# Four 32-column tiles of the matmul array for the layer-3 products of a four-layer graph attention kernel

## The chip, the cores and the metric

The kernel runs on one core of one Trainium2 chip. The metric is the device time of one execution in microseconds (us). Runs of one kernel agree here within about 0.2%.

The profile shows four engines at work. In the kernel before, TensorE (PE) has 12678 matmuls and as many weight loads (PEld), VectorE (DVE) 4595 instructions, ScalarE (ACT) 3009 and GpSimd (POOL) 1455. I call the operand of a weight load the stationary one and the other the moving one: in the rows of line 526 they are 128x65 (LDWEIGHTS) and 128x512 (MATMUL).

## The reference, cut to what matters

Sixteen graphs of 1024 nodes with 256 features go through four attention layers. The first three have one head of 256 values. The fourth, layer 3, has four heads of 64:

```python
h = jnp.einsum('bnd,hde->bhne', nodes_embed, W)            # 4 heads, 64 values each
...
weight = jnp.where(node_adj[:, None] == 0, NEG, weight)
attention = jax.nn.softmax(weight, axis=-1)
dst = jnp.einsum('bhij,bhje->bhie', attention, h) + bias[None, :, None, :]
out = jax.nn.relu(dst) + h                                 # then a norm per head
```

The softmax is done as a weighted sum divided by the sum of the weights. So each target node needs 64 sums of values and one sum of weights per head. These products are in f32.

## The kernel before

Two streams of batches run interleaved: even and odd batches are Python generators. They yield a planned cost, and the one with less planned time is advanced next. `LAG` is the planned start of the second stream. A scheduler then fixes the order of the instructions on each engine.

The weights of a head are eight tiles of 128 source nodes by 1024 targets, made by VectorE (line 317). Layer 3 multiplies them in line 526. The 65 columns of `V3` (64 values and the weight factor) are the stationary operand, and half of the targets is the moving one:

```python
for n in range(H * NH):                       # 4 heads x 2 halves of the targets
    h, g = divmod(n, NH)
    ...
    accT = accumulator(b)[: E + 1, :]         # 65 partitions x 512
    for j in range(NI):                       # 8 source blocks
        if n == 0:
            next(behind)                      # VectorE: the next block's weights
        nc.tensor.matmul(                     # line 526
            accT, V3[:, j, h, :], weights[h * NI + j][:, ts(g, HALF)],
            start=(j == 0), stop=(j == NI - 1),
        )
        ...
    nc.scalar.copy(sums, accT)
    ...
    for i in range(NG):                       # back to targets on partitions
        nc.tensor.transpose(acc[:, i, :], sums[:, ts(i, P)], ident[: E + 1, : E + 1])
    inverse(inv, acc[:, :, E])
    nc.vector.tensor_mul(y[:, ts(g, NG), h, :], acc[:, :, :E], inv...)
```

Of the kernel before, what the change touches and what calls it, by code (L numbers as in the profile page):

```python
# [32 lines left out]
F32 = mybir.dt.float32  # L33
# [5 lines left out]
ALU = mybir.AluOpType  # L39
AX = mybir.AxisListType  # L40

P = 128
# [17 lines left out]
def short_path(ctx: ExitStack, tc: tile.TileContext, ins: dict, out: bass.AP, bad: bass.AP):  # L60

    nc = tc.nc
    x, adj = ins["x"], ins["adj"]
    B, N, D = x.shape
    H, T, E = ins["L3_a_src"].shape
    NI = N // P
    NK = D // P
    HALF = 512
    NH = N // HALF
    NG = HALF // P  # L70
    EXT = [3, 3, 3, 3 * H]
    LAG = 120.0
    ROOT_D = D**0.5
    ROOT_E = E**0.5

# [3 lines left out]
    wide = ctx.enter_context(tc.tile_pool(name="wide", bufs=2))  # L79
    psum = ctx.enter_context(tc.tile_pool(name="psum", bufs=2, space=bass.MemoryType.PSUM))  # L80
    dram = ctx.enter_context(tc.tile_pool(name="dram", bufs=1, space=bass.MemoryType.DRAM))

    ident = const.tile([P, P], F32, name="ident")
# [23 lines left out]
    def load(b: int):  # L107


        narrow = narrows[b % 2]  # L110
        rows = narrow.bitcast(U8).rearrange("(c t q) j -> c q t j", t=2, q=P)
        for c in range(NI // 2):
            cast = nc.gpsimd.dma_start(
                rows[c], adj[b, ts(c, 2 * P), :].rearrange("(q t) j -> q t j", t=2)
            )
            tc.keep_in_program_order(cast)
        if b < 2:
            fetch_nodes(b)
        yield

        mask = masks[b] = nodes.tile([P, NI // 2, N, 2], U8, name="mask")
        for c in range(NI // 2):
            turn = nc.sync.dma_start_transpose(
                mask[:, c].rearrange("p n t -> p (n t)").bitcast(BF), narrow[:, ts(c, P)]
            )
            tc.keep_in_program_order(turn)
            yield
        if b > 1:
            fetch_nodes(b)
            yield  # L130

    def test(b: int):

        for i in range(NI):

            adj_i = adjs.tile([P, N], BF, name="adj_i")
            fetch = nc.gpsimd.dma_start(adj_i, adj[b, ts(i, P), :])  # L137
            if b == 0:
                tc.keep_in_program_order(fetch)


            square = nc.scalar.activation(  # L142
                adj_i, adj_i, AF.Square, bias=minus_half, accum_out=squares[:, b, i : i + 1]
            )
            tc.keep_in_program_order(square)
            yield
# [4 lines left out]
    small = ctx.enter_context(tc.tile_pool(name="small", bufs=6))  # L151
# [104 lines left out]
    def inverse_root(squared: bass.AP, n: int, elements: int, eps: float) -> bass.AP:  # L256

        r = small.tile([P, n], F32, name=f"rstd{n}")
        nc.gpsimd.tensor_scalar_add(r, squared, elements * eps)  # L259
        nc.gpsimd.tensor_tensor(r, r, minus_half.to_broadcast([P, n]), op=ALU.pow)  # L260
        return r

    def accumulator(b: int) -> bass.AP:
        return psum.tile([P, HALF], F32, name=f"acc{b % 2}")
# [40 lines left out]
    def weigh(b: int, column, c, op, into: list):  # L305


        while row_taken:
            yield 0.25
        row_taken.append(b)  # L310
        r = psum.tile([P, N], F32, name="row", bufs=1)
        for i in range(NI):
            nc.tensor.transpose(r[:, ts(i, P)], column(i).to_broadcast([P, P]), ident)  # L313
        yield 0.5
        for j in range(NI):
            w = edges.tile([P, N], F32, name=f"weights{b % 2}")
            nc.vector.scalar_tensor_tensor(w, r, c(j), masks[b][:, j // 2, :, j % 2], op0=op, op1=ALU.mult)  # L317
            into.append(w)
            if j == NI - 1:
                row_taken.pop()  # L320
            yield 0.5

    def start(behind, b: int):

        for t in behind:
            if row_taken == [b]:
                return
            yield t

    def inverse(inv: bass.AP, total: bass.AP):  # L330

        nc.vector.tensor_scalar_max(inv, total, TINY)  # L332
        nc.vector.reciprocal(inv, inv)  # L333
# [14 lines left out]
    def batch(b: int):  # L348
# [3 lines left out]
        coming = load(b + 2) if b + 2 < B else iter(())  # L352
        testing = test(b)
# [18 lines left out]
        last = {}  # L372
# [84 lines left out]
        sums = small.tile([P, NI], F32, name="sums_of_x")  # L457
# [16 lines left out]
        V3 = yield from attend(2, V, finish, 3)  # L474
# [3 lines left out]
        y = single.tile([P, NI, H, E], F32, name="y")  # L478
        normed = []
        shape = [P, NI, E]  # L480

        def center(h: int):

            yh = y[:, :, h, :]
            head = ts(h, E)
            nc.gpsimd.tensor_add(yh, yh, bias[:, head].unsqueeze(1).to_broadcast(shape))  # L486
            nc.vector.scalar_tensor_tensor(yh, yh, 0.0, h3[:, :, head], op0=ALU.max, op1=ALU.add)  # L487
            mean = small.tile([P, NI], F32, name="mean")
            nc.vector.tensor_reduce(mean, yh, AX.X, ALU.add)
            nc.vector.tensor_scalar_mul(mean, mean, 1.0 / E)  # L490
            nc.vector.tensor_sub(yh, yh, mean.unsqueeze(2).to_broadcast(shape))
            square = wide.tile(shape, F32, name="wide", bufs=1)
            nc.scalar.activation(square, yh, AF.Square)
            var = small.tile([P, NI], F32, name="var")
            nc.vector.tensor_reduce(var, square, AX.X, ALU.add)
            return yh, head, inverse_root(var, NI, E, L3_EPS)

        def rescale(yh: bass.AP, head, rstd: bass.AP):
            nc.vector.tensor_mul(yh, yh, rstd.unsqueeze(2).to_broadcast(shape))
            nc.gpsimd.tensor_mul(yh, yh, gamma[:, head].unsqueeze(1).to_broadcast(shape))  # L500
            nc.gpsimd.tensor_add(yh, yh, xb[:, :, head])

        weights = []

        def weigh3(h: int):
            if h == H:
                return iter(())
            return weigh(
                b, lambda i: ex[:, i, 2 * H + h : 2 * H + h + 1],
                lambda j: ex[:, j, H + h : H + h + 1], ALU.max, weights,  # L510
            )

        behind = weigh3(0)
        yield from start(behind, b)
        for n in range(H * NH):
            h, g = divmod(n, NH)
            if g == NH - 1:

                behind = weigh3(h + 1)
                yield from start(behind, b)  # L520

            accT = accumulator(b)[: E + 1, :]
            for j in range(NI):
                if n == 0:
                    next(behind)
                nc.tensor.matmul(  # L526
                    accT, V3[:, j, h, :], weights[h * NI + j][:, ts(g, HALF)],
                    start=(j == 0), stop=(j == NI - 1),
                )
                if n > 0:  # L530
                    next(behind, None)
                yield 0.9
            for _ in behind:
                pass
            sums = wide.tile([E + 1, HALF], F32, name="sums")
            nc.scalar.copy(sums, accT)  # L536
            next(testing)
            next(coming, None)
            yield 0.5
            acc = psum.tile([P, NG, E + 1], F32, name="misc")  # L540
            for i in range(NG):
                nc.tensor.transpose(acc[:, i, :], sums[:, ts(i, P)], ident[: E + 1, : E + 1])  # L542
            inv = small.tile([P, NG], F32, name="inv4")
            inverse(inv, acc[:, :, E])
            nc.vector.tensor_mul(
                y[:, ts(g, NG), h, :], acc[:, :, :E], inv.unsqueeze(2).to_broadcast([P, NG, E])
            )
            yield 0.5
            if g == NH - 1:
                if h > 0:  # L550
                    rescale(*normed.pop())
                normed.append(center(h))
                yield 1.0
        for _ in coming:
            pass
        rescale(*normed.pop())
# [8 lines left out]
    def stream(first: int):  # L565
        for _ in loading[first]:
            yield 2.0
        for b in range(first, B, 2):
            yield from batch(b)
# [3 lines left out]
    next(preparing)  # L573
    streams = [[0.0, stream(0)], [LAG, stream(1)]]
    while streams:
# [311 lines left out]
def tile_gat4(  # L887
# [27 lines left out]
    nc.vector.memset(ones, 1.0)  # L915
    n_bad = flags.tile([1, 1], I32, name="n_bad")
    short_path(tc, ins, out, bad)
    with tc.tile_pool(name="flag_psum", bufs=1, space=bass.MemoryType.PSUM) as psum:
        bads = psum.tile([1, 1], F32, name="bads")
# [39 lines left out]
```

## Time and profile before

The median is 3115.27 us (3113.33 to 3118.95, three runs).

A pass is one matmul instruction of the trace. Each f32 product of layer 3 shows as two passes: 1024 products, 2048 passes.

| what | before |
|---|---|
| TensorE busy | 96% of the span, 98% in mid-kernel |
| VectorE busy | 68% |
| passes of the layer-3 product | 2048, 0.429 us apart |
| passes of layers 0 to 2 (line 408) | 6144, 0.217 us apart |
| TensorE waiting for VectorE's weights | 34 us in all |

A busy TensorE says little about what a change of its work is worth, because matmuls overlap: one of line 526 lasts 592 ns, and the next starts after 429. What counts is the distance between the starts of successive passes. The prediction shows these lines and reads them.

I use one account throughout. I took the start times of all matmuls of a trace and charged each pass the spacing that it has in a dense stream. Each edge between tiled and ordinary passes is charged as read further down, and what remains between the starts counts as waits. The rest of the span lies before the first and after the last matmul. For the kernel before: 2899.3 us of streaming, 177.2 of waits and 38.1 outside, together 3114.6 of a span of 3114.5.

### The profile page before, as it was taken

Reading aid. Unit: us, or ns where it says so; the run is one execution under the profiler, and the core shown is the slowest. Engines: PE = TensorE matmul, PEld = TensorE weight load, DVE = VectorE, ACT = ScalarE, POOL = GpSimd, SP = SyncE. Lnnn points to the kernel's source line nnn. Section 1 sums busy time; section 2 is a strip of 40 time slices with the busy share of each in tenths; the row PEclk is TensorE's granted clock in tenths of the full one; section 3 lists DMA queues with packets and bytes.
Section 4 is the critical chain, followed back from the end, with each engine's and each line's share of the span. In section 5 each row is a group of like instructions: output and inputs, shape, how many; then the busy total and the mean of one; then the engine's idle time right before and its main releaser. Section 6 shows DMA issues by size and latency. Waiting matters only on the chain.

```text
span 3114.5 us, 36472 instructions
## 1 busy us (share of the span) xinstructions
PE 2991.3 (96%) x12678; PEld 2054.2 (66%) x12678; DVE 2113.3 (68%) x4595; ACT 1112.7 (36%) x3009; POOL 961.1 (31%) x1455
## 2 busy tenths in 40 slices
PE   7999999999999999999999999999999999999985
PEld 6775766767576576766757667675765757667552
DVE  5666686666866658676675866768667585766755
ACT  2433334343342433424333343432424334343331
POOL 2123323233242323323233232332323233232333
PEclk9999999999999999999999999999999999999998
DMA  7103122030222203122031220302212131010101
GB/s 124 31 7 52 37 29 53 8 48 28 31 51 21 36 29 45 35 27 55 4 48 31 28 55 7 46 30 31 51 17 38 31 45 34 14 29 4 21 20 26
DMA packets 120462, 105.58 MB, mean 34 GB/s; under 512 B 73680, under 2 KB 91216, under 8 KB 120272
## 3 DMA queue, kind: packets, MB, share of 16 engines
q0 software_dynamic: 40448, 67.12, 14.7%
q1 hardware_dynamic: 79824, 36.05, 5.3%
q8 instruction: 103, 1.69, 0.2%
q14 instruction: 87, 0.71, 0.1%
HBM read 153.49 MB, written 33.55 MB: 60 GB/s over the span
## 4 chain that ended last, share of the span: by engine, by line
PE 76%; DVE 15%; ACT 3%; POOL 3%; issue 3%; DMA 1%; SPq 0%; DVEq 0%; ACTq 0%; POOLq 0%
PE acc L408 36%; PE acc L526 22%; PE acc L296 12%; DVE weights L317 8%; PE misc L289 3%; PE row L313 2%; ACT square L280 1%; PE misc L542 1%; POOL y L486 1%; DVE V L364 1%; DVE x_b L344 1%; POOL rstd L260 1%; DVE x_b L343 1%; ACT below L340 1%; DVE y L487 1%
## 5 line engine op out<-in xcount | busy, mean ns | idle before, releaser
L408 PE MATMUL acc<-V,weights 128*128 128x257 f32 x6144 | 1458.7, 385 | 45.5 <-DVE weights L317 32.5
L408 PEld LDWEIGHTS acc<-V,weights 128*128 128x128 f32 x6144 | 1148.1, 191 | 365.9 <-DVE weights L317 113.7
L526 PE MATMUL acc<-weights,V 128*65 128x512 f32 x2048 | 955.3, 592 | 1.9 <-DVE weights L317 1.5
L317 DVE SCALAR_TENSOR_TENSOR weights<-row,ex,mask 128x1024 f32<-128x1024 f32 x512 | 629.6, 1278 | 11.4 <-PE row L313 11.0
L296 PE MATMUL acc<-W,hT 128*128 128x259 f32 (+1 forms) x2048 | 512.9, 389 | 21.1 <-ACT hT L291 12.9
L526 PEld LDWEIGHTS acc<-weights,V 128*65 128x65 f32 x2048 | 273.3, 138 | 363.0 <-issue 316.4
L317 DVE SCALAR_TENSOR_TENSOR weights<-row,V,mask 128x1024 f32<-128x1024 f32 x384 | 479.6, 1278 | 46.2 <-PE row L313 46.2
L296 PEld LDWEIGHTS acc<-W,hT 128*128 128x128 f32 x2048 | 379.3, 191 | 141.2 <-ACT hT L291 45.6
L280 ACT ACTIVATE square<-x_b,minus_mean 128x256 bf16<-128x256 f32 x512 | 261.0, 510 | 299.7 <-DVE minus_mean L270 288.0
L340 ACT ACTIVATE below<-acc,inv 128x256 f32<-128x256 f32 x256 | 121.1, 473 | 639.7 <-DVE inv L333 517.3
L260 POOL TENSOR_TENSOR rstd<-rstd,minus_half 128x2 f32<-128x2 f32 (+1 forms) x320 | 302.0, 944 | 21.9
L137 POOL DMA_DIRECT2D adj_i<-in_adj_dram x128 | 77.6, 606 | 640.6 <-ACT adj_i L142 628.9
L259 POOL TENSOR_SCALAR rstd<-squared 128x2 f32<-128x2 f32 x256 | 63.3, 247 | 587.4 <-ACT square L280 587.3
L291 ACT ACTIVATE hT<-misc 128x512 f32<-128x512 f32 x256 | 148.4, 596 | 224.9 <-PE misc L289 224.3
L332 DVE TENSOR_SCALAR inv<-acc 128x1 f32<-128x1 f32 x256 | 39.1, 156 | 274.0 <-PE acc L408 272.0
L273 DVE TENSOR_SCALAR centered<-x_b,minus_mean 128x256 f32<-128x256 f32 x512 | 163.7, 365 | 60.2 <-PE misc L289 56.3
L343 DVE SCALAR_TENSOR_TENSOR x_b<-below,x_b 128x256 f32<-128x256 f32 x256 | 125.3, 489 | 103.2 <-ACT below L340 102.9
L360 ACT ACTIVATE V<-acc,rstd 128x3 f32<-128x3 f32 x384 | 99.5, 262 | 244.0 <-PE acc L296 243.8
L289 PEld LDWEIGHTS misc<-ident,centered 128*128 128x128 f32 x1024 | 123.5, 141 | 83.8 <-issue 44.5
L289 PE MATMUL misc<-ident,centered 128*128 128x128 f32 x1024 | 153.7, 276 | 17.3 <-DVE centered L273 17.3
L364 DVE TENSOR_SCALAR V<-acc,rstd,V 128x256 f32<-128x256 f32 x256 | 134.6, 541 | 48.5 <-ACT V L360 47.8
L536 ACT COPY sums<-acc 65x512 f32<-65x512 f32 x128 | 74.1, 579 | 247.2 <-PE acc L526 247.2
(73 smaller groups left out, 2166.4 us busy)
## 6 DMA issues: line engine op xcount, KB each, us to landing
adj_i<-in_adj_dram POOLq DMA_DIRECT2D x128, 256.0 KB, 3.9
x_b<-in_x_dram SPq DMA_DIRECT2D x16, 1024.0 KB, 6.5
narrow<-in_adj_dram POOLq DMA_DIRECT2D x64, 256.0 KB, 9.4
out_dram<-y POOLq DMA_DIRECT2D x32, 512.0 KB, 7.6
mask<-narrow SPq DMA_TRANSPOSE x64, 3.9
W<-in_L_gnn_W_dram SPq DMA_DIRECT2D x3, 256.0 KB, 6.3
weights<-in_L_gnn_a_dram SPq DMA_DIRECT2D x3, 256.0 KB, 8.0
W<-in_L_gnn_W_dram SPq DMA_DIRECT2D x2, 128.0 KB, 7.9
```

Of the source, the lines that this page charges most:

```text
L260: nc.gpsimd.tensor_tensor(r, r, minus_half.to_broadcast([P, n]), op=ALU.pow)
L273: nc.vector.tensor_scalar(centered[:, n, :], xb[:, 2 * pair + n, :], minus_mean[:, n : n + 1], 0.0, op0=ALU.add, op1=ALU.max,)
L280: nc.scalar.activation(square, xb[:, 2 * pair + n, :], AF.Square, bias=minus_mean[:, n : n + 1], accum_out=squared[:, n : n + 1],)
L289: nc.tensor.transpose(turned[:, k, ts(n, P)], centered[:, n, ts(k, P)], ident)
L291: nc.scalar.mul(hT, turned, ROOT_D)
L296: nc.tensor.matmul(projected, hT[:, k, ts(n, P)], W[l][:, k, :], start=(k == 0), stop=(k == NK - 1),)
L317: nc.vector.scalar_tensor_tensor(w, r, c(j), masks[b][:, j // 2, :, j % 2], op0=op, op1=ALU.mult)
L340: nc.scalar.activation(below, acc[:, :D], AF.Exp, scale=inv)
L343: nc.vector.scalar_tensor_tensor(xi, below, 1.0, xi, op0=ALU.min, op1=ALU.add)
L364: nc.vector.tensor_scalar(V[:, i, :D], projected[:, :D], rstd, V[:, i, D : D + 1], op0=ALU.mult, op1=ALU.mult,)
L408: nc.tensor.matmul(accs[i], weights[j][:, ts(i, P)], V[:, j, : D + 1], start=(j == 0), stop=(j == NI - 1),)
L526: nc.tensor.matmul(accT, V3[:, j, h, :], weights[h * NI + j][:, ts(g, HALF)], start=(j == 0), stop=(j == NI - 1),)
```

## The change

The 65-column product (128*65 in the page) is half as wide as those of line 408 (128*128). After the change the array is addressed as four tiles of 32 columns. Each source block gives four products of 32 values (two halves of the targets, two halves of the values), one per tile. The sums of weights become products of their own, with the weight column broadcast to 32. Four source blocks' products are emitted together. The planned units are adapted, so `LAG` goes from 120 to 111.

```diff
-    LAG = 120.0
+    LAG = 111.0
+    QUAD = P // 4
...
+        def in_tiles(parts, accT: bass.AP, first: bool, last: bool):
+            for n, (values, moving) in enumerate(parts):
+                made = nc.tensor.matmul(
+                    accT[ts(n, QUAD), :], values, moving, start=first, stop=last
+                )
+                if pinned:
+                    tc.keep_in_program_order(made)
+                pinned.append(made)
...
+        def add_values(h: int, j: int):
+            for n in (j + 1, j):
+                parts = [
+                    (V3[:, n, h, ts(e, QUAD)], moving)
+                    for moving in halves_of(h, n)
+                    for e in range(2)
+                ]
+                in_tiles(parts, acc, n == 1, n == NI - 2)
+        def add_totals(h: int, j: int):
+            parts = [
+                (V3[:, j + n, h, E:].to_broadcast([P, QUAD]), halves_of(h, j + n)[g])
+                for g, n in ((0, 1), (0, 0), (1, 1), (1, 0))
+            ]
+            in_tiles(parts, total, j == 0, j == NI - 2)
...
+            step = 4
+            for first in range(0, NI, step):
+                pinned = []
+                for j in range(first, first + step, 2):
+                    add_totals(h, j)
+                    if h > 0:
+                        add_values(h, j)
+                for _ in range(step):
+                    next(behind, None)
+                yield 1.8 if h == 0 else 5.4
```

The two accumulators (`acc`, `total`) are then copied, transposed as full 128-row tiles, and normalised once per head on VectorE instead of once per half.

More of the change, by code (lines that the diff above doesn't have):

```diff
@@ L511, in weigh3, with halves_of @@
             )
+        def in_tiles(parts, accT: bass.AP, first: bool, last: bool):
[6 more added lines that the diff above has]
+                pinned.append(made)
+        def halves_of(h: int, j: int):
+            return [weights[h * NI + j][:, ts(g, HALF)] for g in range(NH)]
@@ L513, in batch @@
         behind = weigh3(0)
         yield from start(behind, b)
-        for n in range(H * NH):
-            h, g = divmod(n, NH)
-            if g == NH - 1:
-                behind = weigh3(h + 1)
-                yield from start(behind, b)
-            accT = accumulator(b)[: E + 1, :]
-            for j in range(NI):
-                if n == 0:
-                    next(behind)
-                nc.tensor.matmul(
-                    accT, V3[:, j, h, :], weights[h * NI + j][:, ts(g, HALF)],
-                    start=(j == 0), stop=(j == NI - 1),
-                )
-                if n > 0:
+        for h in range(H):
+            acc = accumulator(b)
+            total = accumulator(b)
+            if h == 0:
+                for j in range(0, NI, 2):
+                    next(behind)
+                    next(behind)
+                    pinned = []
+                    add_values(h, j)
+                    yield 1.8
+                for _ in behind:
+                    pass
+            behind = weigh3(h + 1)
+            yield from start(behind, b)
+            step = 4
+            for first in range(0, NI, step):
+                pinned = []
+                for j in range(first, first + step, 2):
+                    add_totals(h, j)
+                    if h > 0:
+                        add_values(h, j)
+                for _ in range(step):
@@ L531, in batch @@
                     next(behind, None)
-                yield 0.9
+                yield 1.8 if h == 0 else 5.4
             for _ in behind:
                 pass
-            sums = wide.tile([E + 1, HALF], F32, name="sums")
-            nc.scalar.copy(sums, accT)
-            next(testing)
-            next(coming, None)
+            copies = []
+            for accT in (acc, total) if h == 0 else (total, acc):
+                copies.append(wide.tile([P, HALF], F32, name="sums"))
+                nc.scalar.copy(copies[-1], accT)
+                next(testing)
+                next(coming, None)
@@ L539, in batch @@
+            sums, totals = copies if h == 0 else copies[::-1]
             yield 0.5
-            acc = psum.tile([P, NG, E + 1], F32, name="misc")
+            turned = psum.tile([P, NG, P], F32, name="misc")
             for i in range(NG):
-                nc.tensor.transpose(acc[:, i, :], sums[:, ts(i, P)], ident[: E + 1, : E + 1])
-            inv = small.tile([P, NG], F32, name="inv4")
-            inverse(inv, acc[:, :, E])
+                nc.tensor.transpose(turned[:, i, :], totals[:, ts(i, P)], ident)
@@ L545, in batch @@
+            inv = small.tile([P, NH, NG], F32, name="inv8")
+            nc.vector.tensor_reduce(
+                inv, turned[:, :, ::QUAD].rearrange("p i (g n) -> p g i n", n=2), AX.X, ALU.add
+            )
+            inverse(inv, inv)
+            turned = psum.tile([P, NG, NH, E], F32, name="misc")
+            for i in range(NG):
+                nc.tensor.transpose(
+                    turned[:, i].rearrange("p g e -> p (g e)"), sums[:, ts(i, P)], ident
+                )
             nc.vector.tensor_mul(
-                y[:, ts(g, NG), h, :], acc[:, :, :E], inv.unsqueeze(2).to_broadcast([P, NG, E])
+                y[:, :, h, :].rearrange("p (g i) e -> p g i e", g=NH),
+                turned.rearrange("p i g e -> p g i e"),
+                inv.unsqueeze(3).to_broadcast([P, NH, NG, E]),
@@ L547, in batch @@
             )
             yield 0.5
-            if g == NH - 1:
-                if h > 0:
-                    rescale(*normed.pop())
-                normed.append(center(h))
-                yield 1.0
+            if h > 0:
+                rescale(*normed.pop())
+            normed.append(center(h))
+            yield 1.0
         for _ in coming:
```

## The prediction

The prediction's charge for switching is the author's estimate: of the 592 ns of a pass of line 526, 592 - 429 = 163 ns lie under its successor, and entering and leaving the tiling are each charged with these, 0.326 us a run. The kernel before has no tiled pass, so neither this nor the overlap of tiles could be read from its trace, and the 15% for tiles that do not overlap is a judgement.

> **What bounds the kernel now.** I read the engine shares first, then a stretch in mid-kernel, then the groups, then the chain, and the waits last.
>
> The shares and three groups of the page:
> ```profile
> PE 2991.3 (96%) x12678; PEld 2054.2 (66%) x12678; DVE 2113.3 (68%) x4595; ACT 1112.7 (36%) x3009; POOL 961.1 (31%) x1455
> ...
> L408 PE MATMUL acc<-V,weights 128*128 128x257 f32 x6144 | 1458.7, 385 | 45.5 <-DVE weights L317 32.5
> ...
> L526 PE MATMUL acc<-weights,V 128*65 128x512 f32 x2048 | 955.3, 592 | 1.9 <-DVE weights L317 1.5
> ...
> L526 PEld LDWEIGHTS acc<-weights,V 128*65 128x65 f32 x2048 | 273.3, 138 | 363.0 <-issue 316.4
> ```
> TensorE is busy for 96% of the span and the next engine, VectorE, for 68%. Line 526 is the layer-3 product, the one the change rewrites. It needs 16 batches x 4 heads x 2 halves x 8 blocks = 1024 products, and the row has 2048 instructions: an f32 product runs as two passes, each with its own weight load. The row also shows the waste: 128*65 means that 65 of the array's 128 columns are used.
>
> Four hundred microseconds in the middle, all instructions, then line 526 alone (columns: stretch, its length, busy time of each engine):
> ```profile
> 1000.00:1400.00 400.00, 392.08 (x1672) 268.98 (x1671) 282.53 (x608) 145.07 (x392) 128.86 (x192) 1.00 0.23 36
> ...
> 1000.00:1400.00 400.00, 129.90 (x279) 37.42 (x280) 1.00 0.23 36
> ```
> In steady state TensorE is busy for 98% at full clock, and a third of that is line 526. Two batches run interleaved, so one batch's layer 3 lies beside another's earlier layers.
>
> A busy time from modelled ends is not a cost. The cost is the distance from one start to the next, and the chain that ended last gives it (start, length, what):
> ```profile
> 1440.59 4.29 PE acc L526 x10
> ...
> 1493.91 6.93 PE acc L408 x32
> ...
> 1528.94 0.87 PE row L313 x8
> ```
> 4.29 / 10 = 0.429 us for a pass of 512 moving columns, 6.93 / 32 = 0.217 us for 257, and 0.109 us for a transpose of 128. A matmul's own duration is 592 ns, so 592 - 429 = 163 ns of each lies under its successor. Line 526 thus costs 2048 x 0.429 = 879 us of TensorE. TensorE does wait for someone, but little:
> ```profile
> PE acc L408 <- DVE weights L317: 32.5, 41, 1.7
> PE misc L289 <- DVE centered L273: 17.3, 16, 12.0
> PE acc L296 <- ACT hT L291: 12.9, 21, 1.0
> ```
> So a microsecond taken from the TensorE stream should come off the end nearly whole, until VectorE's 68% comes near.
>
> [...]
>
> **The change part by part.**
>
> *Removed:* 1024 full-array products, 2048 passes, 879 us. Also 512 transposes of a 65-row tile, whose 65 moving columns follow each other at about 60 ns: 31 us.
>
> *Added, streaming:* per head, each of 8 source blocks gives four products of 32 values (two halves of the targets by two halves of the 64 values). The sums of weights, formerly the 65th column, become products of their own: 2 halves x 8 blocks, with the weight column broadcast to 32. That is 32 + 16 = 48 products, dealt to four tiles, or 12 per tile, two passes each. If the four tiles stream together a head needs 24 pass times instead of 32. Over 64 heads the ideal is 64 x 24 = 1536 pass times. The scheduler cuts some groups of four apart. I counted in the compiled changed program, run of tiled passes by run, the passes on the fullest tile: 1606 in all. 1606 x 0.429 = 689 us. The transposes become 512 of 128 columns: 512 x 0.109 = 56 us. Stream balance: 689 + 56 - 879 - 31 = -165 us.
>
> *Added, switching:* the compiled program has 324 separate runs of tiled passes, about 20 a batch. The lengths are mostly 8, 16 and 48 passes: four source blocks are held together in heads 1 to 3, but head 0 is fed block by block as VectorE makes the weights, and other work cuts in between. Every run enters and leaves the tiling. [...] A first load may be exposed as well. Loads are 138 ns for 65 columns and 191 for 128 (the LDWEIGHTS rows), so by straight line about 111 for 32. Worst case: 0.33 + 0.11 + 0.19 = 0.63 us a run, 204 us in all. With hidden loads: 324 x 0.326 = 106 us. I take this second figure, because the trace shows loads hidden everywhere else. It is a choice, not a measurement.
>
> *VectorE:* per head before, two of each: a clamp at 156 ns, a reciprocal at 176, a multiply of 256 elements at 421, or 1.51 us. After: one reduction of some 0.25 us (estimate, from the 172 ns of the smallest reductions), clamp and reciprocal 0.33, one multiply of 512 at 0.69 (as the other 512-element operations): 1.27 us. That is 64 x 0.24 = 15 us less, off the path. ScalarE still copies two tiles of 512 per head at 579 ns. GpSimd does not change.
>
> *Moved:* before, a head used one accumulator at a time and the other was being filled. Now values and totals hold both, so this stream's next head waits for one or two copies (0.58 us each). The other stream usually fills that time. I charge 15 us for 64 heads, about 0.23 us each.
>
> Sum: -165 + 106 + 15 = -44 us, so 3071 us, rounded to 3070. The shift of the second stream's start (120 to 111 in the program's own planning units) is half of the shortened plan of a batch, and I give it nothing by itself.
>
> **The rivals.**
>
> *Tiles do not overlap[...].* In the compiled program the two passes of a product stand side by side on the same tile: first pass tile 0, second pass tile 0, first pass tile 1, and so on. If matmuls must also start in program order, the second pass of tile 0 holds back tile 1, and only two passes overlap. Counted over the same 324 runs that is 3400 pass times, 1459 us instead of 689, and the kernel would take over 3700 us. [...] a plan that holds 24 products together makes little sense without overlap. Some 15%.
>
> *Switching eats the gain.* With 0.51 us a run the 165 us are gone; with 0.63 us the kernel is 3115 - 165 + 204 + 15 = 3169 us. For it: 324 runs are many, and those in head 0 contain only two groups of four. [...]
>
> *Switching is almost free*, only the stream counts: 3115 - 165 + 15 = 2965 us. That is the good end; the waits of TensorE on VectorE would grow a little, as VectorE rises to about 71%.
>
> *VectorE becomes the bound:* 2098 us of work against 2965 says no over the whole. Locally, eight weight rows at 1.28 us are 10.2 us a head, against 10.3 us of ideal tiled streaming, so head 0 may wait. That would show as tens of microseconds at most.
>
> **Range and chances.** Independent tiles with cheap to dear switching give 2965 to 3169. [...] The in-order case lies far above, or partly so if overlap is imperfect. I put the range at 2945 to 3300, which leaves room below for better packing between the two streams and cuts off the far tail. Faster by over 2% (below 3053): 0.42. Within 2%: 0.33. Slower by over 2% (above 3178): 0.25.
>
> **What would show it.** Tiles together: within a held run the four tiles' passes start close together, and 24 products span about 12 x 0.429 = 5.1 us; 10 us or more would mean the in-order rival. Switching: the gap between the last tiled pass's start and the next full-array start beyond 0.429 us, and the reverse on entering; I expect some 0.16 us each. Line 408 must keep 0.217 us a pass and the granted clock must stay at 1.00, or another effect is at work. Waits of TensorE on the weights should remain below 60 us. The prediction is wrong if tiled passes on different tiles space out at 0.2 us or more, or if a switch costs above 0.5 us.

## The result

The changed kernel takes 3024.82 us (3023.68 to 3025.67, four runs) against 3114.86 us in the same rounds. The ratio is 0.9709 (95% interval 0.9692 to 0.9726): faster by 2.9%. Ratios are the mean time of one kernel's fast runs over that of the other's of the same rounds, so not quite the ratio of the medians. The prediction had 3070 us. The measured time is inside its range, but the forecast gain of 45 us was half of the real 90 us.

The shares and the same groups of the page of the changed kernel (line 517 is now the layer-3 product, 409 is the old 408):
```profile
PE 2905.2 (96%) x16774; PEld 1960.1 (65%) x16774; DVE 2112.7 (70%) x4467; ACT 1092.1 (36%) x3009; POOL 964.5 (32%) x1455
...
L409 PE MATMUL acc<-V,weights 128*128 128x257 f32 x6144 | 1452.5, 386 | 24.6 <-ACT above L343 12.8
...
L517 PE MATMUL acc<-weights,V 128*32 128x512 f32 x6144 | 756.4, 598 | 3.6 <-DVE weights L318 3.6
...
L517 PEld LDWEIGHTS acc<-weights,V 128*32 128x32 f32 x6144 | 174.1, 109 | 379.6 <-issue 370.6
```
The layer-3 product now has three times as many passes, each as long as before (598 against 592 ns), and is busy for 756 us instead of 955. One after the other, 6144 passes at 0.429 us would take 2636 us, so passes run at the same time. The loads of 32 columns take 109 ns, where the prediction had estimated 111. TensorE is still busy for 96%, and 78% of the chain that ended last lies on it (76% before).

The same stretch in mid-kernel, all instructions and then line 517 alone:
```profile
1000.00:1400.00 400.00, 393.26 (x2321) 261.66 (x2320) 284.40 (x596) 151.38 (x411) 134.05 (x196) 1.00 0.23 36
...
1000.00:1400.00 400.00, 110.48 (x912) 25.85 (x912) 1.00 0.23 36
```
TensorE's busy time (393.26 of 400 us, 392.08 before) and granted clock (1.00) are those of before. Layer 3's part fell from 129.9 to 110.5 us of 400, although the batches also come faster. Of the four such stretches from 600 to 2200 us this one shows the smallest fall: over all four the mean fell from 130.5 to 101.5. And TensorE's longest waits, whose counterparts the prediction shows:
```profile
PE acc L297 <- ACT hT L292: 28.2, 19, 1.8
PE misc L290 <- DVE centered L274: 13.8, 4, 13.0
PE acc L409 <- ACT above L343: 12.8, 17, 1.6
PE bads L973 <- DVE bad L644: 11.5, 1, 11.5
PE acc L409 <- DVE weights L318: 7.6, 5, 2.8
```
The wait of line 409 on VectorE's weights fell from 32.5 to 7.6 us, and the one on ScalarE's `hT` rose from 12.9 to 28.2. Over the whole list (which holds about half of the waits of the account) VectorE's waits fell from 62 to 44 us and ScalarE's rose from 29 to 48, so the sum stayed.

Two entries and exits of the layer-3 product in the kernel before, and one held group (source blocks emitted together) after, from the timelines of TensorE (start, length, what):
```profile
839.82 1.03 PE L408 MATMUL acc<-V,weights 128*128 128x257 f32 x4
840.69 1.02 PE L526 MATMUL acc<-weights,V 128*65 128x512 f32 x2
...
845.15 1.02 PE L526 MATMUL acc<-weights,V 128*65 128x512 f32 x2
846.01 1.25 PE L408 MATMUL acc<-V,weights 128*128 128x257 f32 x5
```
```profile
840.06 0.60 PE L290 MATMUL misc<-ident,centered 128*128 128x128 f32 x4
840.59 5.36 PE L517 MATMUL acc<-weights,V 128*32 128x512 f32 x48
845.87 1.35 PE L409 MATMUL acc<-V,weights 128*128 128x257 f32 x5
```
Three things can be read in the group after. First, 48 passes on four tiles take 845.87 - 840.59 = 5.28 us from start to the next start, where one after the other they would take 48 x 0.429 = 20.6 us. Twelve pass times are 5.15 us. Second, on entering: the four transposes of 0.109 us from 840.06 would let the next pass start at 840.50, and it starts at 840.59, so 0.09 us are lost. Third, on leaving: 5.28 - 5.15 = 0.13 us. By the list of all starts 0.02 of it is that the four tiles start some 7 ns apart, and 0.02 that the first pass of a run is followed after 453 ns instead of 429; the rest, 0.09, is lost at the edge. Where nothing is waited for, these figures are constant over the trace. After the last tiled pass the next ordinary one starts 523 ns later (429 and 94). The first tiled pass starts 310 ns after a 257-column pass (217 and 93) or 202 ns after a transpose (109 and 93). It makes no difference whether a transpose or a 257-column pass follows, though their loads take 141 and 190 ns.

The change of shape alone costs nothing. In the lines of before, line 526 starts 840.69 - 839.82 = 0.87 us after four 257-column passes (4 x 0.217), and line 408 starts 846.01 - 845.15 = 0.86 us after two passes of line 526 (2 x 0.429). Over that trace the median spacings are 217 and 429 ns in 213 and 233 such pairs. So the 0.09 us come with the tiling.

The account, before and after:

| us | before | after | change |
|---|---|---|---|
| layer-3 passes | 878.4 | 701.9 | -176.5 |
| other passes | 2020.9 | 2045.2 | +24.3 (wider transposes) |
| entering and leaving the tiling | 0 | 60.6 | +60.6 (324 runs x 0.187) |
| waits between matmuls | 177.2 | 181.6 | +4.4 |
| before the first, after the last matmul | 38.1 | 34.0 | -4.1 |
| sum | 3114.6 | 3023.3 | -91.3 |

A "run" here and below is a stretch of tiled passes with no other matmul between them. It is counted in the compiled program, and so is the number of passes on the fullest tile, summed over the runs. One of the 324 is a closing check's product (line 973), which also addresses a 32-column tile.

### The profile page after: what moved, and what is told of

It is laid out like the page before. It is cut to its first block, busy times and chain, and to the rows that moved or that the text cites. A ratio compares the mean times of both kernels' runs of the same rounds, so it can differ in the third digit from the quotient of the medians.

```text
span 3023.3 us, 44588 instructions
## 1 busy us (share of the span) xinstructions
PE 2905.2 (96%) x16774; PEld 1960.1 (65%) x16774; DVE 2112.7 (70%) x4467; ACT 1092.1 (36%) x3009; POOL 964.5 (32%) x1455
## 4 chain that ended last, share of the span: by engine, by line
PE 78%; DVE 12%; POOL 4%; ACT 4%; issue 2%; DMA 1%; SPq 0%; ACTq 0%; POOLq 0%; DVEq 0%
PE acc L409 39%; PE acc L517 21%; PE acc L297 11%; DVE weights L318 6%; PE misc L290 3%; PE row L314 2%; POOL rstd L261 2%; POOL y L487 1%; DVE y L500 1%; DVE V L365 1%; DVE var L496 1%; PE misc L594 1%; ACT adj_i L143 1%; ACT square L281 1%; PE misc L586 1%
## 5 line engine op out<-in xcount | busy, mean ns | idle before, releaser
L409 PEld LDWEIGHTS acc<-V,weights 128*128 128x128 f32 x6144 | 1135.1, 190 | 338.3 <-DVE weights L318 92.7
L517 PE MATMUL acc<-weights,V 128*32 128x512 f32 x6144 | 756.4, 598 | 3.6 <-DVE weights L318 3.6
L297 PE MATMUL acc<-W,hT 128*128 128x259 f32 (+1 forms) x2048 | 522.1, 391 | 39.8 <-ACT hT L292 28.2
L517 PEld LDWEIGHTS acc<-weights,V 128*32 128x32 f32 x6144 | 174.1, 109 | 379.6 <-issue 370.6
L389 POOL TENSOR_TENSOR x_b<-x_b,beta 128x256 f32<-128x256 f32 x128 | 93.6, 731 | 491.1 <-ACT square L281 491.1
L579 ACT COPY sums<-acc 128x512 f32<-128x512 f32 x128 | 75.0, 586 | 413.9 <-PE acc L517 413.9
L274 DVE TENSOR_SCALAR centered<-x_b,minus_mean 128x256 f32<-128x256 f32 x512 | 180.4, 383 | 4.3
L344 DVE SCALAR_TENSOR_TENSOR x_b<-below,x_b 128x256 f32<-128x256 f32 x256 | 117.7, 460 | 87.6 <-ACT below L341 87.4
L290 PE MATMUL misc<-ident,centered 128*128 128x128 f32 x1024 | 159.7, 278 | 15.7 <-DVE centered L274 13.8
```

Of the source, the lines that this page charges most:

```text
L274: nc.vector.tensor_scalar(centered[:, n, :], xb[:, 2 * pair + n, :], minus_mean[:, n : n + 1], 0.0, op0=ALU.add, op1=ALU.max,)
L290: nc.tensor.transpose(turned[:, k, ts(n, P)], centered[:, n, ts(k, P)], ident)
L297: nc.tensor.matmul(projected, hT[:, k, ts(n, P)], W[l][:, k, :], start=(k == 0), stop=(k == NK - 1),)
L344: nc.vector.scalar_tensor_tensor(xi, below, 1.0, xi, op0=ALU.min, op1=ALU.add)
L409: nc.tensor.matmul(accs[i], weights[j][:, ts(i, P)], V[:, j, : D + 1], start=(j == 0), stop=(j == NI - 1),)
L517: made = nc.tensor.matmul(accT[ts(n, QUAD), :], values, moving, start=first, stop=last)
```

## The experiments

The theory is the account: streaming, plus 0.207 us for each run (0.187 of switching and 0.02 for the tiles' staggered start), and nothing else. The longer first pass was overlooked; with it a run costs 0.227 us. Rivals: the shifted start of the second stream made the gain; switches are free at the end; switches are dearer; another engine is already near.

### The shift of the second stream, in the kernel before

```diff
-    LAG = 120.0
+    LAG = 111.0
```

> The kernel before with the second stream's start moved from 120 to 111 planning units, nothing else. Theory (the whole gain of 90 us is TensorE's: 152 us less streaming, 61 us more switching): the shift alone is worth nothing, 3115 us within 10. Rival (the better interleaving of the two streams brought part of the gain): 3070 to 3095 us.

Measured: 3117.82 us against 3116.47, ratio 1.0006 (0.9990 to 1.0023). The order on TensorE did change, but waits stayed at 177.2 us. The shift alone is worth nothing in the kernel before.

### The shift undone, in the changed kernel

```diff
-    LAG = 111.0
+    LAG = 120.0
```

> The changed kernel with the second stream's start put back to 120. Its compiled program has 248 separate runs of tiled passes instead of 324, and 1638 passes on the fullest tile (summed over the runs) instead of 1606. Theory, with 0.429 us a pass and 0.207 us a run (0.187 of switching, 0.02 of skew): 3025 + 32 x 0.429 - 76 x 0.207 = 3023 us, within 10. Rival (the shift was needed): 3045 us or more.

Measured: 3080.39 us, ratio 0.9884 (0.9867 to 0.9900). The theory missed by 57 us, and the rival is right that the shift was needed. Streaming (2759.3 us) and switching (46.3 us) came as computed. The waits rose from 182 to 240 us. The longest waits of TensorE in this run:
```profile
PE acc L297 <- DVE V L365: 31.0, 14, 2.7
PE misc L290 <- DVE centered L274: 27.3, 15, 13.4
PE acc L409 <- DVE weights L318: 14.4, 11, 1.4
```
All three lie on VectorE. In the changed kernel they were 6.3, 13.8 and 7.6 us. What goes with them is seen in the stores of the finished batches, which alternate between the two streams. From the timeline of the changed kernel (start, length, what):
```profile
682.37 1.56 POOL L611 DMA_DIRECT2D out_dram<-y  x2
866.40 1.56 POOL L611 DMA_DIRECT2D out_dram<-y  x2
1050.42 1.56 POOL L611 DMA_DIRECT2D out_dram<-y  x2
1234.44 1.56 POOL L611 DMA_DIRECT2D out_dram<-y  x2
```
and of this run:
```profile
1068.67 1.56 POOL L611 DMA_DIRECT2D out_dram<-y  x2
1278.05 1.56 POOL L611 DMA_DIRECT2D out_dram<-y  x2 [0.30 <-POOL y L502]
1442.14 1.56 POOL L611 DMA_DIRECT2D out_dram<-y  x2
1651.51 1.56 POOL L611 DMA_DIRECT2D out_dram<-y  x2 [0.30 <-POOL y L502]
```
The changed kernel finishes a batch every 184 us: the two streams are half a period apart. This run has 209 and 164 us in turn, and keeps to that until the end. Before the change the distances were 187 to 193 us, at either start. So the theory needs a second part: the waits are small only while the streams stay half a period apart.

### Two source blocks held together

```diff
-            step = 4
+            step = 2
...
-                yield 1.8 if h == 0 else 5.4
+                yield 0.9 if h == 0 else 2.7
```

> The changed kernel with two source blocks held together instead of four (planning units per step halved with it). Compiled: 383 runs, 1634 passes on the fullest tile. Theory: 3025 + 28 x 0.429 + 59 x 0.207 = 3049 us. Rival (a switch costs nothing at the end, as it falls where TensorE waits anyway): 3025 + 12 = 3037 us or less. Rival (a switch costs 0.5 us or more): 3067 us or more.

Measured: 3059.61 us, ratio 0.9819 (0.9803 to 0.9836). Streaming rose by some 14 us and switching by 11, as computed; waits rose by 8. The streams stayed even (186 us). This lies between the theory and the dear switch, so it excludes free switches but does not settle the price.

### Eight source blocks held together, start at 105

```diff
-    LAG = 111.0
+    LAG = 105.0
...
-            step = 4
+            step = 8
...
-                yield 1.8 if h == 0 else 5.4
+                yield 3.6 if h == 0 else 10.8
```

> Eight source blocks held together and the second stream's start at 105. Compiled: 190 runs, 1632 passes on the fullest tile. Theory: 3025 + 26 x 0.429 - 134 x 0.207 = 3008 us. Rival (switches free): 3036 us. Rival (a longer hold starves the other stream, so waits of TensorE grow): over 3030 us with TensorE's waits up by more than 20 us.

Measured: 3059.99 us, ratio 0.9817 (0.9801 to 0.9834). Switching fell to 35.4 us, as computed, but waits were 236 us. The third rival is right in its number, not in its reason: the outputs are 172 and 200 us apart in turn, so this is the uneven phase again. The run at 111 with eight blocks, below, tells the two apart.

### Starts of 108, 114, 110 and 100

```diff
-    LAG = 111.0
+    LAG = 108.0      # and 114.0, 110.0, 100.0
```

> The changed kernel with the second stream's start at 108 instead of 111. Compiled: 317 runs, 1610 passes on the fullest tile, so streaming and switching are as before to 1 us. Theory as it stands after the run at 120 (where waits of TensorE between matmuls were 240 us against 182 at 111, with streaming and switching as predicted): the waits depend on how the scheduler interleaves the two streams, and 108 keeps the interleaving of 111, so 3025 us within 15. Rival (111 is a lucky single point): 3045 us or more.

> The second stream's start at 114. Compiled: 251 runs, 1636 passes on the fullest tile, nearly the pattern of 120. Theory: the pattern decides, so the waits are those of the run at 120, and the time is 3080 us within 20. Rival (the waits grow smoothly with the distance from 111): 3035 to 3050 us.

> The changed kernel with the second stream's start at 110. Compiled: 324 runs, 1608 passes on the fullest tile, the same pattern. Expected with the pattern's waits (182 to 186 us at 111 and 108): 3026 us within 6. If it is outside, the waits are not set by the pattern of runs.

> The second stream's start at 100. Compiled: 242 runs, 1632 passes on the fullest tile, the pattern of fewer runs, like 114 and 120. If that pattern comes with 218 to 240 us of waits as it did there: streaming and switching 3025 + 11 - 17 = 3019, plus 36 to 58 us, so 3055 to 3077 us. Rival (the waits belong to the start time, not to the pattern): anything from 3015 us on, and with 182 us of waits it would be the best kernel, 3019 us.

| start | us, ratio | outputs apart | waits | runs |
|---|---|---|---|---|
| 100 | 3071.68, 0.9864 | 173 / 200 | 234 | 242 |
| 108 | 3028.78, 0.9717 | 184 | 186 | 317 |
| 110 | 3027.13, 0.9724 | 184 | 183 | 324 |
| 111 | 3024.82, 0.9709 | 184 | 182 | 324 |
| 114 | 3059.35, 0.9817 | 173 / 200 | 218 | 251 |
| 120 | 3080.39, 0.9884 | 164 / 209 | 240 | 248 |

111 is no lucky single point: 108 to 111 give the same within 4 us. The time jumps when the phase becomes uneven, in both directions, and then costs 36 to 58 us of waits. The run at 114 missed narrowly: 3059 us, where 3060 to 3100 was expected and the rival had 3035 to 3050. Its waits are 218 us, not the 240 of the run at 120. Why the scheduler falls into an uneven phase at one start and not at another was not tested. The uneven phase has fewer runs, so its order is different in detail too.

### Eight source blocks held together, start at 111

```diff
-            step = 4
+            step = 8
...
-                yield 1.8 if h == 0 else 5.4
+                yield 3.6 if h == 0 else 10.8
```

> Eight source blocks held together, at the changed kernel's own start of 111. Compiled: 308 runs, 1634 passes on the fullest tile. With the waits of the changed kernel (182 us between matmuls): 3025 + 28 x 0.429 - 16 x 0.207 = 3034 us. Rival (any other order of the program costs waits, as the runs at 105, 114 and 120 did): 3055 us or more. Only below 3015 us would it be a better kernel.

Measured: 3031.29 us, ratio 0.9735 (0.9719 to 0.9751), with even outputs (184 us) and 180 us of waits. A longer hold does not starve the other stream. It is no better kernel, as it saves only 16 runs and cuts groups less evenly.

### Most of the sums of weights left out (wrong on purpose)

```diff
-            in_tiles(parts, total, j == 0, j == NI - 2)
+            if j == 0:
+                in_tiles(parts, total, True, True)
...
-            inverse(inv, inv)
+            nc.vector.tensor_scalar_max(inv, inv, 0.5)
+            nc.vector.reciprocal(inv, inv)
```

> The changed kernel with only the first two source blocks' sums of weights (wrong denominators on purpose, floored at 0.5, so a wrong result). Compiled: 234 runs, 1246 passes on the fullest tile. If TensorE's stream is what sets the end: 3025 - 360 x 0.429 - 90 x 0.207 = 2852 us, within 25 for other waits. Rival (VectorE, 2113 us of work, is already close enough that part of it turns into waits): 2900 us or more.

Measured: 2917.75 us, ratio 0.9364 (0.9348 to 0.9380), and a wrong result. The rival is right. Streaming fell by 159 us and switching by 17, but waits rose by 67, with even outputs (177 us). The page's shares:
```profile
PE 2750.8 (94%) x15238; PEld 1921.9 (66%) x15238; DVE 2118.7 (73%) x4467; ACT 1092.2 (37%) x3009; POOL 958.9 (33%) x1455
```
and its longest waits:
```profile
PE acc L409 <- DVE weights L318: 34.2, 50, 2.8
PE acc L297 <- ACT hT L292: 31.0, 19, 3.3
PE misc L290 <- DVE centered L274: 25.3, 18, 12.0
```
VectorE has the same work in less time, and TensorE waits for it more: over the whole list 88 us instead of 44, with ScalarE's waits down from 48 to 43. Of the 176 us saved on TensorE only some 60% (107 us) came off the end.

### The products of a held group given tile by tile

```diff
-                made = nc.tensor.matmul(
-                    accT[ts(n, QUAD), :], values, moving, start=first, stop=last
-                )
+                waiting.append((n, accT[ts(n, QUAD), :], values, moving, first, last))
...
+        def flush():
+            for n, to, values, moving, first, last in sorted(waiting, key=lambda m: m[0]):
+                made = nc.tensor.matmul(to, values, moving, start=first, stop=last)
+                ...
+            waiting.clear()
```
with `flush()` at the end of each held group.

Two outcomes are open in what was expected: 48 passes still take 5.3 us, or they take 12 to 20 us.

> The changed kernel with the products of a held group given tile by tile: all of tile 0, then all of tile 1, and so on, so in a run of 48 passes 12 in a row go to the same tile. [...] tile 1 starts within some 0.1 us of tile 0 and 48 passes still take 5.3 us. If a tile can hold only a few waiting instructions, tile 1 starts after most of tile 0's passes, and 48 passes take 12 to 20 us; the kernel then takes 3700 us or more. By the runs alone (341 runs, 2246 passes on the fullest tile, since they are cut differently) it would take 3025 + 640 x 0.429 + 17 x 0.207 = 3303 us.

Measured: 4058.8 us (one run, state unknown, correct). From its timeline:
```profile
1589.53 15.72 PE L524 MATMUL acc<-weights,V 128*32 128x512 f32 x48
```
The same 48 passes take 15.7 us instead of 5.3. In the list of starts, with the tiles told apart by program order, tile 1's first pass begins 6 ns after tile 0's ninth of twelve, when three of tile 0's passes were still to start. If the same holds from each tile to the next, the run takes 8 + 8 + 8 + 12 = 36 pass times, 15.4 us (an estimate), and the timeline has 1605.19 - 1589.53 = 15.66 to the next start. Where only four passes in a row go to one tile (the runs of 16 in this kernel), 16 passes still take 1.87 us, against 1.85 in the changed kernel. So the in-order rival of the prediction is half true. With twelve passes in a row to one tile, program order held the next tile back (15.7 us); with four (1.87 us) or the two of one product (1.85 us) it did not. By what mechanism was not shown.

### Added cuts, and their control

The price of a switch at the end of the kernel was still open, because runs and phase had changed together. Both kernels below have 192 added products of a zero stationary operand with one moving column, which add zero to an accumulator. In the first each cuts a run of tiled passes; in the second four stand together after each head's first held group.

```diff
+            made = nc.tensor.matmul(
+                to[:, 0:1], zeros.to_broadcast([P, P]), weights[h * NI + j][:, 0:1], start=False, stop=False
+            )
...
                     if h > 0:
+                        add_zero(h, j, acc if j == NI - 2 else total)     # first kernel
                         add_values(h, j)
+                if h > 0 and first == 0:                                   # second kernel
+                    for _ in range(NI // 2):
+                        add_zero(h, 0, acc)
```

> The changed kernel with 192 added full-array products with a stationary operand of zeros and one moving column, each set between the totals and the values of a pair of source blocks in heads 1 to 3, so that each cuts a run of tiled passes in two (the result stays right). Compiled: 529 runs, 1722 passes on the fullest tile; the control has 355 and 1662. Theory (a run costs 0.207 us, and this reaches the end): 174 x 0.207 + 60 x 0.429 = 62 us over the control. Rival (switching hidden at the end): 26 us. Rival (0.5 us a run, as the break-even in the prediction): 113 us.

> The control: the same 192 products of zeros, four together after each head's first held group, where they cut little. Compiled: 355 runs, 1662 passes on the fullest tile. At 0.22 to 0.25 us each (two passes with a load of 128 columns): 3025 + 45 + 56 x 0.429 + 31 x 0.207 = 3100 us, within 20, if the two batches stay half a period apart (outputs 184 us apart, not 164 and 209).

Measured: 3156.50 us (ratio 1.0125) and 3093.28 us (ratio 0.9923). The difference is 63 us; the theory had 62, the rivals 26 and 113. The outputs stay even in both (193 and 189 us), and the control came within its expected 3100 +- 20. It is 68 us above the changed kernel; with 24 for its 56 more passes and 6 for its 31 more runs, some 38 us are left for the 192 products, 0.20 us each (an estimate from these two runs, if waits are unchanged), where 0.22 to 0.25 had been estimated. In the account streaming differs by 31 us (groups cut apart), switching by 33, and waits by less than 1. So both the cut groups and the switch at 0.187 us reach the end whole.

### A build that needed no run

Leaving out the lines that pin the tiled products to program order gives, on every engine, exactly the same order of instructions. In this program the pinning holds nothing together. That they are emitted together is what is left to do it; this was not tested by itself.

## Why the prediction was right or wrong

*That TensorE's stream sets the end* was right: TensorE stays at 96%, and the account closes on it.

*That tiles overlap* was right. The predicted 5.1 us for 24 products were 5.28 with the stagger, the longer first pass and the edge on leaving.

*The streaming term, -165 us,* was right in its parts: 1606 passes on the fullest tile, wider transposes. It missed 13 us, 0.04 us in each of 324 runs (staggered start and longer first pass); the measured term is -152 us.

*The switching term, 106 us, was mis-sized, and this is the step that failed.* The prediction took the 163 ns hidden under a matmul's successor as exposed twice, 0.326 us a run. It measured 0.094 us at each edge, 0.187 us a run, so 61 us. With the 13 us inside the runs it is 74. Why an edge costs 94 ns and not 163 is not shown. The choice that loads stay hidden agrees with the trace: the edge is 93 or 94 ns, whether the load after it takes 109 ns (32 columns), 141 (a transpose) or 190 (line 409).

*The charge of 15 us for the two accumulators* did not show. The waits between matmuls rose by 4.4 us in all, and the only wait listed before line 517 is 3.6 us on weights, none on a copy. That the accumulators cost nothing is not shown: ScalarE, which makes the copies, was waited for 19 us more elsewhere, VectorE 18 us less, and no run separates the causes.

*The sum.* -165 + 13 + 61 + 4 - 4 = -91 us instead of -44. The 45 us of switching that did not come are nearly the whole difference of 47; the 13 us that streaming cost more and the 15 less of waits and outside almost cancel, which is luck.

*That the shift of the second stream is worth nothing by itself* was right for the kernel before and wrong as a statement about the change: with the tiled layer the old start costs 55 us. The prediction never asked whether the streams would stay half a period apart, and the full gain came only because the new start kept them there. At the old start the changed kernel takes 3080 us, close to the predicted 3070 by luck: smaller switching and larger waits would have cancelled. That the phase goes with the waits is shown in six starts. By what path it makes them was not shown. In the lists of waits of the four uneven runs VectorE's sum is 67 to 92 us, against 44 in the changed kernel, and ScalarE's is 34 to 47, against 48.

*VectorE* fell by 17 us in the normalisation (predicted 15), from 96.4 to 79.5 us by the groups, and was no bound. Its busy time as a whole did not fall (2113.3 and 2112.7 us), as others of its groups took longer: line 274, the old 273, went from 163.7 to 180.4 us. In the run with fewer sums it is what TensorE waits for most (88 us, 44 in the changed kernel).

No variant beat the changed kernel; its neighbours at 108 and 110 are the same within 4 us.

## What to carry to other kernels

Here a product of 65 columns was cut into column tiles of 32 with profit (2.9%) although the cut tripled the passes. Consecutive products went to different tiles (given tile by tile the kernel took 4058.8 us), and the tiled passes came in runs of mostly 8 to 48, at 0.187 us of switching a run. Count the runs and the passes on the fullest tile in the compiled program before predicting. When two streams share the engines, look at the distances of their outputs first; a change that shortens one stage can move the phase, and an uneven phase here cost 36 to 58 us of waits, nearly as much as all the switching (61). Once the first engine has been relieved by some per cent, do not count on the next saving on it in full: here 107 of 176 us came off the end.
